# Sixteen copies of cached values ahead of the first head group, weight loads in halves, and a new set of early products in a one-core residual stack

## The chip, the core and the metric

The kernel runs on one core of a Trainium2 chip, as one program in one launch. The metric is the device time of that launch in microseconds (us), the median over several runs. All arithmetic is 32-bit float.

## The reference

Four residual layers are applied in turn to `x`, 64 sequences of 32 positions with 512 features:

```python
# per-sequence channel mix, weights picked by itok_B_0_15
x = x + einsum('bct,bcd->bdt', x, L0_weights[cond])
# linear layer with a LoRA, picked by itok_B_6_15
h = einsum('bsd,brd->bsr', x, A[adapter])
x = x + (einsum('bsd,od->bso', x, base_w) + bias + einsum('bsr,bor->bso', h, B[adapter]))
# attention over a paged cache: 32 query heads, 8 key/value heads of 128, 16 pages of 32 keys
q, k, v = x @ Wq.T, x @ Wk.T, x @ Wv.T
q, k = rope(rmsnorm(q)), rope(rmsnorm(k))
keys = concat(k_cache[block_table], k); values = concat(v_cache[block_table], v)
p = softmax(where(valid, q @ keys.T * SCALE, -1e30))   # a cached key is valid below cache_seqlen
x = x + (p @ values) @ Wo.T
# per-sequence channel mix once more
x = x + einsum('bct,bcd->bdt', x, L3_weights[cond])
```

A sequence has 512 cached keys and 32 new ones, and every key/value head serves four query heads.

## The kernel before

**Tiles and groups.** The 2048 positions are 16 tiles of 128 rows, four sequences to a tile. The eight key/value heads are two groups of four (`g` is 0 or 1), and the attention runs over all tiles for group 0 and then for group 1. A *unit* is one sequence and one group, 128 units in all. A unit has four *periods* (the code calls them slots), one for each key/value head, so there are n = 512 periods. Eight units, that is two tiles or 32 periods, are a *pair*; pairs 0 to 7 are group 0, pairs 8 to 15 group 1.

**A plan written by hand.** Each piece of work is put into a period with `at(slot, where, ...)`, and `slot(i)` sends the pieces of a period out in a fixed order: "fetch", "pool", scores, transpositions of the probabilities, "pe", "power", "turn", values, "dve", "keep", "act", "store". Each engine works through its own instructions in that order. SyncE (SP) issues the ordinary transfers and GpSimd (POOL) the indirect ones, also in program order.

**A period of attention.** `Unit.scores` multiplies the queries of one head by all keys (L808, L811). One instruction on VectorE (DVE) adds the mask `pen` and takes the minimum, `top` (L816). ScalarE (ACT) takes the exponential (L827), and `divide` scales it (L833). `Unit.flip` transposes the probabilities (L850) and DVE copies them out of PSUM (L852). `Unit.values` multiplies them by the values three periods behind the scores (L863). The masks are made on POOL by `Unit.mask` (L779), for a unit three periods ahead of its first score.

**Where keys and values come from.** `Turn` takes 128 cached keys of one group, transposes them on PE, and `Turn.store` writes them to DRAM page by page (`kT_dram`). For group 0 the sixteen turns lie in front, for group 1 one turn goes with each tile of group 0. For group 1, `Turn.store` also copies the values of its 128 cached rows into `v_dram`, in which a row holds the values of all four heads of the group (L281). A unit's keys come as sixteen ordinary transfers of one page each (L759). Its values come as indirect loads of 128 rows each (`gather`, L105), four times 128 keys. In group 1 that is one gather of 512 numbers per row from `v_dram`. In group 0 there are two gathers per 128 keys, each of 256 numbers per row (one pair of heads), from the cache as it came in; their row numbers are the tables `rows["pair", 0]` and `rows["pair", 1]`, made in front. The table for group 1 is made in the middle (`second_rows`). The loaded values have eight buffers (`v_sb`), two units' worth.

**Projections beside the attention.** During pair i the projections of pair i+1 run on the same PE: `Plain.project` for keys and values (L555), `Block.project` for the queries (L622, by a scheme of seven products for eight), whose weight sums are made by `block_sum` on DVE. `Norm` normalizes and rotates the heads; its `power` step runs on POOL (L679) and waits for DVE's `ss` (L677).

**Front.** The first two layers (`First`) run tile by tile before and beside the projections of pair 0. Their x tiles are loaded on SP (L382), from `begin`, the first period of all. The weights of group 0 are loaded there as well: v's and k's after the second x tile's place in the plan, and all of q's at once behind the second period.

**Weights.** The weight buffers `w0` to `w8` are used three times: for group 0, for group 1 (loaded during pair 7) and for the output weights wo (loaded during pair 15). The loads are whole tiles of 1 MB (k's and v's as two of 512 KB), put at the start of a period ("fetch").

**End.** The output projection also forms seven products for eight, per pair of tiles: p1 to p7, each of 16 matmuls with 256 columns. For the first pair of tiles three of them, p1, p2 and p7, are made early, spread over the last 24 periods (`early_product`, L1110); their inputs `o_in` are loaded 27 periods before the end, all four at once, and `early_sums` combines them on DVE. The rest is made behind the periods (L1281), with the last channel mix (`mixed`) of a pair behind the next pair's p1.

## Time and profile before

| | us |
|---|---|
| median of 3 runs (2548.47 to 2557.93) | 2554.17 |
| profiled execution, its own time | 2682.29 |
| its span, first to last instruction | 2680.5 |
| PE busy in the span | 2522.0 (94%) |
| DVE busy | 1663.5 (62%) |
| POOL busy | 1331.2 (50%) |
| ACT busy | 1287.0 (48%) |
| start of the first score matmul | 207.1 |
| start of group 1's first score matmul | 1319.6 |
| gathers of group 0's values, 512 | 519.0 |
| gathers of group 1's values, 256 | 261.3 |

Busy time is the sum over an engine's instructions. A row of a group names line, engine, operation, tiles (written <- read) and count, then busy time and mean ns of one, then the idle time before these instructions and what ended it. The span of the one profiled execution is longer than the median of the runs without a profile by 126 us; sums in this document that are made from its rows are compared with its own time.

### The profile page before, as it was taken

To read this page: it belongs to the slowest core of one execution; us is meant where nothing else is said; L and a number is where in the kernel's file an instruction comes from. 1 tells how busy PE (TensorE), PEld (TensorE's weight loads), DVE (VectorE), ACT (ScalarE), POOL (GpSimd) and SP (SyncE) were. 2 spreads that over 40 slices of the span, in tenths; PEclk is the share of its full clock that TensorE was granted. 3 is DMA by queue.
4 is the path that set the end of the run, shared out by engine and by line. 5 is a ranking of instruction groups with operands and counts; after the bars stand their busy time and mean duration, and the time that the engine had idled before them with its cause. 6 is when DMAs were issued, how large, how long until landed. Compare 5 with 4: busy or idle time off the path is not lost.

```text
span 2680.5 us, 47052 instructions
## 1 busy us (share of the span) xinstructions
PE 2522.0 (94%) x13824; PEld 1882.3 (70%) x13824; DVE 1663.5 (62%) x4166; ACT 1287.0 (48%) x3671; POOL 1331.2 (50%) x1136
## 2 busy tenths in 40 slices
PE   6998999999999898989899999999999989999999
PEld 3555666666666666666677777777777767888888
DVE  5655666566666666667667767776777766522322
ACT  1235555556555555556566666666666654100000
POOL 4326666666667666667654555554544544100000
PEclk9999999999999999999999999999999999999999
DMA  7746565556565656575556555665656675323321
GB/s 244 246 155 181 158 183 156 170 163 180 160 179 158 181 154 200 183 218 158 173 167 193 170 180 170 182 181 171 199 167 202 210 264 171 143 79 115 123 79 56
DMA packets 441023, 457.34 MB, mean 171 GB/s; under 512 B 54081, under 2 KB 366273, under 8 KB 430401
## 3 DMA queue, kind: packets, MB, share of 16 engines
q1 hardware_dynamic: 393408, 315.35, 37.6%
q0 software_dynamic: 47360, 138.99, 17.8%
q8 instruction: 112, 1.84, 0.3%
q14 instruction: 143, 1.16, 0.1%
HBM read 382.82 MB, written 75.50 MB: 171 GB/s over the span
## 4 chain that ended last, share of the span: by engine, by line
PE 83%; DVE 6%; DMA 4%; issue 3%; another core or an unknown queue 2%; ACT 2%; SPq 1%; POOL 1%; DVEq 0%; ACTq 0%; POOLq 0%
PE o_ps L863 15%; PE proj_ps L622 14%; PE out_ps L1281 14%; PE s_ps L808 9%; PE proj_ps L555 8%; PE pT_ps L850 7%; PE s_ps L811 7%; PE head_ps L721 2%; PE o_ps L875 2%; PE l_ps L461 2%; DVE pT L852 1%; DVE sm L816 1%; DMA x_sb<-in_x 1%; DVE raw L634 1%
## 5 line engine op out<-in xcount | busy, mean ns | idle before, releaser
L816 DVE CUSTOM_DVE_ANT_0 sm<-s_ps,pen 128x544 f32<-128x544 f32 x512 | 370.5, 724 | 534.3 <-PE s_ps L811 284.8
L863 PEld LDWEIGHTS o_ps<-pT,v_sb 128*128 128x128 f32 x4096 | 526.0, 194 | 148.7 <-issue 135.2
L827 ACT ACTIVATE sm<-sm,top 128x544 f32<-128x544 f32 x512 | 383.5, 749 | 499.1 <-DVE top L816 418.6
L105 POOL DMA_INDIRECT v_sb<-in_kv_cache,pair_rows x512 | 519.0, 1014 | 198.5 <-issue 119.2
L863 PE MATMUL o_ps<-pT,v_sb 128*128 128x128 f32 x4096 | 547.7, 277 | 8.5 <-DMA v_sb<-in_kv_cache,pair_rows 5.3
L833 ACT ACTIVATE sm<-sm,share 128x512 f32<-128x512 f32 x512 | 370.8, 724 | 227.9 <-DVE share L832 190.4
L105 POOL DMA_INDIRECT v_sb<-v,v_rows x256 | 261.3, 1021 | 270.3 <-PE o_ps L863 220.6
L808 PE MATMUL s_ps<-kT,qT 128*128 128x288 f32 x1024 | 351.9, 425 | 36.7 <-DVE top L816 26.3
L852 DVE COPY pT<-pT_ps 128x512 f32<-128x512 f32 x512 | 351.7, 687 | 52.8 <-PE s_ps L811 21.1
L679 POOL TENSOR_TENSOR rstd<-ss,minus_half 128x4 f32<-128x4 f32 x160 | 187.2, 1170 | 383.0 <-DVE ss L677 379.0
L850 PE MATMUL pT_ps<-ident,sm 128*128 128x128 f32 x2048 | 310.6, 275 | 22.0 <-DVE pT L852 15.7
L850 PEld LDWEIGHTS pT_ps<-ident,sm 128*128 128x128 f32 x2048 | 255.5, 141 | 80.4 <-DVE pT L852 15.6
L811 PE MATMUL s_ps<-kT,qT 128*128 128x256 f32 x1024 | 306.3, 381 | 1.7 <-DMA kT<-kT 1.2
L779 POOL TENSOR_SCALAR pen<-key_f,seq_f 128x544 f32<-128x544 f32 x128 | 280.3, 2190 | 13.5 <-DMA x<-xS 2.6
L811 PEld LDWEIGHTS s_ps<-kT,qT 128*128 128x128 f32 x1024 | 195.1, 191 | 57.4 <-DMA kT<-kT 2.3
L105 POOL DMA_INDIRECT mix_rows<-in_w,cond_rows x32 | 40.8, 1275 | 333.3 <-DVE mix_diag L168 293.0
L672 ACT ACTIVATE sq<-raw 128x128 f32<-128x128 f32 x640 | 190.7, 301 | 32.3 <-DVE raw L634 21.6
L808 PEld LDWEIGHTS s_ps<-kT,qT 128*128 128x128 f32 x1024 | 155.5, 192 | 59.4 <-DVE top L816 32.0
L634 DVE TENSOR_TENSOR raw<-proj_ps,raw 128x512 f32<-128x512 f32 x224 | 150.7, 685 | 27.8 <-PE proj_ps L622 25.9
L1281 PE MATMUL out_ps<-w,o_in 128*128 128x256 f32 x768 | 167.1, 379 | 0.0
L1331 ACT COPY p<-out_ps 128x256 f32<-128x256 f32 x7 | 2.6, 373 | 333.1 <-PE out_ps L1281 333.1
L1281 PEld LDWEIGHTS out_ps<-w,o_in 128*128 128x128 f32 x768 | 145.9, 190 | 19.8
(159 smaller groups left out, 3592.9 us busy)
## 6 DMA issues: line engine op xcount, KB each, us to landing
kT<-kT SPq DMA_DIRECT2D x2048, 64.0 KB
o<-oT SPq DMA_DIRECT2D x32, 1024.0 KB
o_in<-o SPq DMA_DIRECT2D x32, 1024.0 KB
rot<-rot SPq DMA_DIRECT2D x48, 256.0 KB
wq<-in_wq SPq DMA_DIRECT2D x8, 1024.0 KB
page_rows<-in_kv_cache SPq DMA_DIRECT2D x32, 256.0 KB
vn<-v_rows SPq DMA_DIRECT2D x32, 256.0 KB
kT<-page_T SPq DMA_DIRECT2D x32, 256.0 KB
```

The costliest lines, as they stand in the source:

```text
L105: nc.gpsimd.indirect_dma_start(out=dst, out_offset=None, in_=table, in_offset=bass.IndirectOffsetOnAxis(ap=index, axis=0),)
L622: nc.tensor.matmul(self.ps, lhsT=self.pair.x[x][:, half][:, c, :], rhs=blocks(self.b)[w][:, c, :], start=(c == 0), stop=(c == 1),)
L779: nc.gpsimd.tensor_scalar(self.pen, key_f, seq_f[:, self.b : self.b + 1], BIG, ALU.is_ge, ALU.mult)
L808: nc.tensor.matmul(ps[:, first:HID], lhsT=q, rhs=self.kT[:, :n1, k, :], start=True, stop=True)
L811: nc.tensor.matmul(ps[:, HID : first + LA], lhsT=q, rhs=self.kT[:, n1:, k, :], start=True, stop=True)
L816: nc.vector.tensor_tensor_reduce(out=sm, in0=ps[:, first : first + LA], in1=self.pen, scale=1.0, scalar=3e38, op0=ALU.add, op1=ALU.min, ac ...
L827: nc.scalar.activation(sm, sm, AF.Exp, bias=top, scale=-1.0, accum_out=total)
L833: nc.scalar.activation(sm[:, :L], sm[:, :L], AF.Copy, scale=share)
L850: nc.tensor.transpose(ps[:, c, :], self.sm[k][:, c * P : (c + 1) * P], ident)
L852: nc.vector.tensor_copy(pT, ps)
L863: nc.tensor.matmul(self.o_ps[k], lhsT=self.v[c][:, k * D : (k + 1) * D], rhs=self.pT[k][:, c, :], start=(c == 0), stop=False,)
L1281: nc.tensor.matmul(ps[:, :HALF], lhsT=o[:, i, :], rhs=w[i // REP][:, i % REP, :], start=(i == 0), stop=(i == KG * REP - 1),)
```

## The change

**Values.** `v_dram` becomes a list of two, and `Turn.store` makes its copy for both groups. So sixteen copies of 256 KB, from the cache to DRAM, come into the front, each ahead of its turn's store of keys. `fetch_values` makes one gather of 512 numbers per row in either group, with one table of row numbers, `v_rows`, made in front; `second_rows` and the two tables for group 0 go.

**Front.** It begins one period later relative to pair 0 (the number 11 becomes 10). The first five x tiles are loaded in the first three periods, two in each. v's weights come with the second period, k's with the third, q's by halves in the following eight.

**Weight loads.** Every weight tile is loaded by two transfers of 512 KB, one per period, at a period's end ("store"). The starts are periods 6, 11, 21, 23, 32, 34, 36 and 38 of the pair's plan (before: 6, 11, 21, 21, 32, 32, 32, 32). The block sums move by one to three periods.

**Last periods.** The three early products are now the p1 of three pairs of tiles, (1, 2, 0) in this order, all with the same output weights w11. Their inputs are loaded by halves, one per period; four of the six tiles loaded are for pair 0, one for each of the others. The third weights are made 19 to 22 periods into the last 24 (before: 8 to 11). The sums of pair 0 are made behind the periods, where pairs 0, 1 and 2 now have six products each and the others seven.

```diff
...
-    def load_kv_weights(g, kind):
-        w = wpool.tile([P, NC, KG * D], F32, name=f"w{'kv'[kind]}{g}", tag=f"w{kind}")
-        for i in (0, 1):
-            nc.sync.dma_start(
-                out=w[:, :, i * 2 * D : (i + 1) * 2 * D],
-                in_=wkv[2 * g + i][:, :, kind * 2 * D : (kind + 1) * 2 * D],
+    def load_kv_weights(g, kind, i):
+        if i == 0:
+            w_sb[kind] = wpool.tile(
+                [P, NC, KG * D], F32, name=f"w{'kv'[kind]}{g}", tag=f"w{kind}"
             )
-        w_sb[kind] = w
-    def load_q_weights(g, k):
-        w_sb["q", k] = wpool.tile([P, NC, REP * D], F32, name=f"wq{g}_{k}", tag=f"w{2 + k}")
-        nc.sync.dma_start(out=w_sb["q", k], in_=wq[KG * g + k])
-    def load_o_weights(k):
-        tag = f"w{(1, 0, 2, 3, 4, 5, 6, 7)[k]}"
-        w_sb["o", k] = wpool.tile([P, REP, HID], F32, name=f"wo{k}", tag=tag)
-        nc.sync.dma_start(out=w_sb["o", k], in_=wo[k])
+        nc.sync.dma_start(
+            out=w_sb[kind][:, :, i * 2 * D : (i + 1) * 2 * D],
+            in_=wkv[2 * g + i][:, :, kind * 2 * D : (kind + 1) * 2 * D],
+        )
+    def load_q_weights(g, k, i):
+        if i == 0:
+            w_sb["q", k] = wpool.tile([P, NC, REP * D], F32, name=f"wq{g}_{k}", tag=f"w{2 + k}")
+        part = slice(i * NC // 2, (i + 1) * NC // 2)
+        nc.sync.dma_start(out=w_sb["q", k][:, part], in_=wq[KG * g + k][:, part])
+    def load_o_weights(k, i):
+        if i == 0:
+            tag = f"w{(1, 0, 2, 3, 4, 5, 6, 7)[k]}"
+            w_sb["o", k] = wpool.tile([P, REP, HID], F32, name=f"wo{k}", tag=tag)
+        part = slice(i * REP // 2, (i + 1) * REP // 2)
+        nc.sync.dma_start(out=w_sb["o", k][:, part], in_=wo[k][:, part])
...
-    v_dram = dram.tile([PAGES * PSIZE, KG * D], F32, name="v_1")
+    v_dram = [dram.tile([PAGES * PSIZE, KG * D], F32, name=f"v_{g}") for g in range(NG)]
...
-                if self.g:
-                    nc.sync.dma_start(
-                        out=v_dram[c * P : (c + 1) * P, :].rearrange("k (i f) -> k i f", i=2),
-                        in_=self.cached(1),
-                    )
+                nc.sync.dma_start(
+                    out=v_dram[self.g][c * P : (c + 1) * P, :].rearrange("k (i f) -> k i f", i=2),
+                    in_=self.cached(1),
+                )
...
-                if self.g:
-                    gather(v, v_dram[:, :], rows["v"][:, at])
-                else:
-                    by_pair = kv_cache.rearrange("r (w f) -> (r w) f", w=2)
-                    for i in (0, 1):
-                        gather(v[:, i * 2 * D : (i + 1) * 2 * D], by_pair, rows["pair", i][:, at])
+                gather(v, v_dram[self.g][:, :], v_rows[:, at])
...
-                at(home - 11, "fetch", make, pair_of, 0, Pair, 0)
+                at(home - 10, "fetch", make, pair_of, 0, Pair, 0)
...
-                sums = [(b, what) for b in (0, 1) for what in (3, 2, 1)] + [(0, 4), (1, 4)]
-                for w, one in enumerate(sums):
-                    at(home + 4 + w, "dve", block_sum, *one)
+                sums = [(b, what) for b in (0, 1) for what in (3, 2, 1, 4)]
+                for w, one in zip((5, 6, 7, 9, 10, 11, 12, 13), sums):
+                    at(home + w, "dve", block_sum, *one)
             if p == NT // 2 - 1:
-                last = g == NG - 1
-                if last:
+                if g == NG - 1:
                     loads = [(load_o_weights, k) for k in range(2 * KG)]
                 else:
                     loads = [(load_kv_weights, g + 1, k) for k in (1, 0)]
                     loads += [(load_q_weights, g + 1, k) for k in range(KG)]
-                for w, load in zip((6, 11, 21, 21, 32, 32, 32, 32), loads):
-                    at(home + w, "fetch", *load)
+                for w, load in zip((6, 11, 21, 23, 32, 34, 36, 38), loads):
+                    for j in (0, 1):
+                        at(home + w + j, "store", *load, j)
...
-        begin = -WINDOW - AHEAD - 11
+        begin = -WINDOW - AHEAD - 10
...
-            home = -WINDOW - AHEAD - 7 + 2 * t
+            home = -WINDOW - AHEAD - 6 + 2 * t
             f = [first_of, t]
-            at(max(begin, home - 5), "fetch", make, *f, First, t)
+            at(home - 5 if t > 4 else begin + t // 2, "fetch", make, *f, First, t)
...
-        def second_rows():
-            rows["v"] = rows_of(const, "v_rows", table, B * NC, PSIZE, lane32_f, tag="rows_0")
-        at(n // 2 - 2, "dve", second_rows)
...
-        def fetch_o(name, g, t):
-            o = o_pools[0].tile([P, KG * REP, P], F32, name="o_in", tag=name)
-            nc.sync.dma_start(out=o, in_=o_dram[g][t])
-            early[name] = o
+        def fetch_o(name, g, t, i):
+            if i == 0:
+                early[name] = o_pools[0].tile([P, KG * REP, P], F32, name="o_in", tag=name)
+            part = slice(i * KG * REP // 2, (i + 1) * KG * REP // 2)
+            nc.sync.dma_start(out=early[name][:, part], in_=o_dram[g][t][:, part])
-        def early_sums(i):
-            a11, a12, a21, a22 = (early[f"a{i}"] for i in (11, 12, 21, 22))
+        def early_product(pair, name, i):
             if i == 0:
-                early["s3"] = wpool.tile([P, KG * REP, P], F32, name="s3", tag="w8")
-            dst, a, op, b = (
-                (early["s3"], a11, ALU.subtract, a21),
-                (a21, a21, ALU.add, a22),
-                (a11, a21, ALU.subtract, a11),
-                (a12, a12, ALU.subtract, a11),
-            )[i]
-            nc.vector.tensor_tensor(dst, a, b, op)
-        def early_product(name, o, first, half, i):
-            if i == 0:
-                early[name] = ps_m.tile([P, HID], F32, name="proj_ps", tag="m")[:, : HID // 2]
+                early["p1", pair] = ps_m.tile([P, HID], F32, name="proj_ps", tag="m")
             nc.tensor.matmul(
-                early[name],
-                lhsT=early[o][:, i, :],
-                rhs=w_sb["o", first + i // REP][:, i % REP, half * HID // 2 : (half + 1) * HID // 2],
+                early["p1", pair][:, : HID // 2],
+                lhsT=early[name][:, i, :],
+                rhs=w_sb["o", i // REP][:, i % REP, : HID // 2],
                 start=(i == 0),
                 stop=(i == KG * REP - 1),
             )
-        def early_keep(name):
-            ps = early[name]
-            early[name] = o_pools[0].tile([P, HID // 2], F32, name=f"{name}_first")
-            nc.scalar.copy(early[name], ps)
+        def early_keep(pair):
+            ps = early["p1", pair]
+            early["p1", pair] = o_pools[0].tile([P, HID // 2], F32, name=f"p1_{pair}")
+            nc.scalar.copy(early["p1", pair], ps[:, : HID // 2])
-        for j, (name, o, k, half) in enumerate(
-            (("p1", "a11", 0, 0), ("p2", "a12", KG, 0), ("p7", "s3", 0, 1))
-        ):
+        for j, (pair, name) in enumerate(((1, "a12"), (2, "a21"), (0, "a11"))):
+            for i in (0, 1):
+                at(home - 3 + 3 * j + i, "store", fetch_o, name, 0, 2 * pair, i)
             for i in range(KG * REP):
-                at(home + 8 * j + i // 2, "pe", early_product, name, o, k, half, i)
-            at(home + 8 * j + 7, "act", early_keep, name)
+                at(home + 8 * j + i // 2, "pe", early_product, pair, name, i)
+            at(home + 8 * j + 7, "act", early_keep, pair)
+        for i in (0, 1):
+            at(home + 9 + i, "store", fetch_o, "a12", 1, 0, i)
+            at(home + 12 + i, "store", fetch_o, "a22", 1, 1, i)
+            at(home + 17 + i, "store", fetch_o, "a21", 0, 1, i)
         for k in range(KG):
-            at(home + 8 + k, "dve", third_weights, k)
-        for i, w in enumerate((5, 13, 15, 17)):
-            at(home + w, "dve", early_sums, i)
+            at(home + 19 + k, "dve", third_weights, k)
...
-            load_kv_weights(0, 1)
-            load_kv_weights(0, 0)
             for i in range(begin + 1, begin + 11):
                 slot(i)
                 for _ in range(2 if i < begin + 6 else 1):
                     next(more, None)
-                if i == begin + 1:
-                    for k in range(KG):
-                        load_q_weights(0, k)
+                c = i - begin - 1
+                if c < 2:
+                    for j in (0, 1):
+                        load_kv_weights(0, 1 - c, j)
+                elif c < 10:
+                    load_q_weights(0, (c - 2) // 2, c % 2)
...
-                    for k in (0, 1):
-                        base = 2.0 * k * PAGES * PSIZE + 1
-                        rows["pair", k] = rows_of(
-                            const, f"pair_rows_{k}", table, B * NC, PSIZE, lane32_f, 2.0, base,
-                            tag=f"rows_{k}",
-                        )
+                    v_rows = rows_of(const, "v_rows", table, B * NC, PSIZE, lane32_f)
...
-                    for name, g, t in (
-                        ("a11", 0, 0), ("a12", 1, 0), ("a21", 0, 1), ("a22", 1, 1)
-                    ):
-                        fetch_o(name, g, t)
...
-                if pair:
+                p1 = early.get(("p1", pair))
+                if p1 is None:
                     p_1 = product(a11, w11)
                     p1 = pool.tile([P, HALF], F32, name="p1")
-                    nc.vector.tensor_tensor(s3, a11, a21, ALU.subtract)
-                    add(a21, a21, a22)
-                    nc.vector.tensor_tensor(a11, a21, a11, ALU.subtract)
-                    for at_last in waiting:
-                        mixed(*at_last)
-                    p_2 = product(a12, w21)
-                    nc.vector.tensor_tensor(a12, a12, a11, ALU.subtract)
-                    p_7 = product(s3, w_3)
-                    p_3 = product(a12, w22)
-                else:
-                    p1, p_2, p_7 = early["p1"], early["p2"], early["p7"]
-                    p_3 = product(a12, w22)
+                nc.vector.tensor_tensor(s3, a11, a21, ALU.subtract)
+                add(a21, a21, a22)
+                nc.vector.tensor_tensor(a11, a21, a11, ALU.subtract)
+                for at_last in waiting:
+                    mixed(*at_last)
+                add(x3[0][:, lo], x3[0][:, lo], p1)
+                add(x3[0][:, hi], x3[0][:, hi], p1)
+                p_2 = product(a12, w21)
+                nc.vector.tensor_tensor(a12, a12, a11, ALU.subtract)
+                add(x3[0][:, lo], p_2, x3[0][:, lo])
+                p_7 = product(s3, w_3)
+                if pair == 0:
...
-                add(x3[0][:, lo], x3[0][:, lo], p1)
-                add(x3[0][:, hi], x3[0][:, hi], p1)
-                add(x3[0][:, lo], p_2, x3[0][:, lo])
...
+                p_3 = product(a12, w22)
                 add(x3[0][:, hi], p_3, x3[0][:, hi])
...
```

## The prediction

> **What bounds the kernel now.** I read the engine shares first: PE is busy 94% of the span, so the question is where the other time goes. The stretches between the starts of the pairs' first score matmuls (found by L808) tell. A pair is 32 periods, the same work sixteen times over; pairs 0 to 7 are the first group, 8 to 15 the second. Columns: stretch, length, then busy us and count of PE, its weight loads, DVE, ACT, POOL; last the granted clock, DMA share and GB/s.
>
> ```profile
> 484.00:622.00 138.00, 127.77 (x722) 92.68 (x721) 89.86 (x238) 79.39 (x227) 93.12 (x83) 0.98 0.57 168
> 1032.40:1178.80 146.40, 128.50 (x723) 92.15 (x721) 88.56 (x235) 79.22 (x227) 94.03 (x84) 0.98 0.64 198
> 1682.40:1803.10 120.70, 120.61 (x714) 89.80 (x713) 89.19 (x234) 77.04 (x225) 62.22 (x51) 1.00 0.61 179
> 2044.60:2170.50 125.90, 120.60 (x710) 89.53 (x709) 88.33 (x234) 77.27 (x225) 64.20 (x53) 0.99 0.69 216
> 2170.50:2291.80 121.30, 108.99 (x699) 93.44 (x698) 75.70 (x181) 59.23 (x133) 44.53 (x36) 0.95 0.61 197
> ```
>
> See that pair 11 (third row) is PE alone: 120.6 of 120.7 us. Pair 2 (first row) needs 138 for the same products. Only POOL differs, 93 us against 62. The eight first-group pairs take 1319.6 - 207.1 = 1112.5 us; pairs 8 to 13 take 725.0, 120.8 each.
>
> POOL's waits in pair 2, then in pair 11 (engine, tile, line waited for: us, times, longest):
>
> ```profile
> POOL rstd L679 <- DVE ss L677: 18.1, 7, 4.2
> POOL v_sb L105 <- issue: 14.8, 51, 0.3
> POOL v_sb L105 <- PE o_ps L863: 10.3, 4, 9.0
> ...
> POOL v_sb L105 <- PE o_ps L863: 23.2, 12, 7.9
> ```
>
> And the groups of POOL in pair 2:
>
> ```profile
> L105 POOL DMA_INDIRECT v_sb<-in_kv_cache,pair_rows x64 | 64.4, 1006 | 27.4 <-issue 14.8 <-PE o_ps L863 10.3 <-PE pT_ps L850 1.3
> L779 POOL TENSOR_SCALAR pen<-key_f,seq_f 128x544 f32<-128x544 f32 x8 | 17.3, 2167 | 0.7
> ```
>
> Per unit (four periods, 15.1 us at PE's pace) POOL issues 8 gathers of 1.006 us with 14.8 / 64 = 0.23 us between, 9.9 us, one mask `pen` of 2.17 and 1.4 `rstd` of 1.15: 13.6 us. It runs in order, so its 18.1 us of waits for DVE's `ss` (2.3 per unit) count: 15.9 us. That is more than PE needs. POOL falls behind, `pen` comes late behind gathers, and the softmax reduction on DVE waits for it:
>
> ```profile
> 503.24 2.10 POOL L779 TENSOR_SCALAR pen<-key_f,seq_f 128x544 f32<-128x544 f32 x1
> 504.75 0.72 DVE L816 CUSTOM_DVE_ANT_0 sm<-s_ps,pen 128x544 f32<-128x544 f32 x1 [3.97 <-remote]
> ```
>
> DVE stood 3.97 us for nothing but this mask. PE then stands too, and its clock halves for 3.4 or 6.8 us after several such gaps (clock 0.98).
>
> **Part 1: one gather per 128 keys.** 256 of 512 gathers go from group 0: per unit 4 x (1.006 + 0.23) = 4.9 us off POOL, leaving about 8.7 plus waits, as in group 1, whose gathers of twice the row are no dearer (1.021 against 1.006 us). What is late next is PE. Group 0 keeps one page transposition per tile that group 1 lacks: 8 of 0.11 us per pair, so 120.7 + 0.9 = 121.6, times 8 = 973 us; 4 us for the reload stretch: 977. Saved: **135 us** of the profiled run.
>
> What it adds: 16 copies of 256 KB from DRAM to DRAM in front, on SP, each between a `page_rows` load and a `kT` store. Group 1's like copies issue in 0.62 us and move in some 2.5 us. In the instruction order each SP transfer waits for the one eight before it. SP has room there (the last kT store issues at 171, the first kT load at 190.6), and DMA is 0.57 busy from 100 to 218; 4 MB more adds about 0.12. Hidden, I cost it at 0. If all 16 issues came onto the path: 10 us. The first gather waits for all 16 copies, but the last is planned ten periods earlier.
>
> **Part 2: the front.** In the first 45 us PE waits for an x tile queued behind 6 MB of weights:
>
> ```profile
> 37.53 2.05 PE L407 MATMUL mix_ps<-x_sb,mix_diag 128*128 128x512 f32 x2 [8.56 <-DMA x_sb<-in_x]
> ```
>
> Now x tiles 2 and 3 issue before the weights, which come at 1 MB a period and later 0.5. The 8.6 us go, and with them the half clock behind (three groups run 2.6 us longer than their equals at 47 us): **-11 us**. The front is one period shorter, but the same products merely overlap differently: 0. The weights are still early: v's are needed some 40 us in. Cover gone: one 0.5 MB part, some 3 us. The row numbers move from four times 16 to one set of 8 small DVE instructions in front and none in the middle: under 2 us, 0. The block sums move by one to three periods on DVE, ahead of their first use: 0 (bounds -3 to +3).
>
> **Part 3: loads in halves, one per period, at the period's end.** At 2120 and 2165 bursts of 2 and 4 MB fill the DMA engines (1.01 busy, 365 and 417 GB/s); kT, v and v_new transfers queue behind. PE is busy 6.67 of 10 us at 2165, 5.72 at 2195, 5.59 at 2215. Pair 6 loses 146.4 - 138 = 8.4 us to q's burst (counted in part 1), pair 14 some 4 of its 5, pair 15 more. Against halves stands a rule: the Trainium skill, "DMA: Bandwidth & Descriptors", section Bandwidth, wants transfers of 1 MiB or more, and its anatomy section gives each about 2.0 us fixed. Twenty 1 MB loads cut in two would by that cost up to 20 x 2 = 40 us. The row says otherwise for this place: eight transfers are in flight, so fixed parts overlap, and it is a saturated stretch (1.01) that PE suffers from. I take 0 for the cut. A steady period needs 0.61 x 3.77 = 2.3 us of DMA; 0.5 MB at the 365 GB/s of the burst adds 1.4: 3.7 of 3.77. It just fits.
>
> **Part 4: the last periods.** Early products stay 48 matmuls of 256 columns, now p1 of three pairs; four third weights stay, the four 2.28 us DVE sums move behind the loop; o_in grows from 4 to 6 MB. Without projections, pair 15's last six units ran at best 13.2 us; the first two carry the wo loads, and at 3.7 us of DMA a period can't go under 15: 30 + 6 x 13.3 = 110, against 121.3: **-11**; pair 14 **-4**. Behind the loop the 53 products stay 53 (48 + 5 before; 6 + 6 + 6 + 35 now). DVE of pair 0: three sums end 6.9 us in, a12 waits for p_2, w_2 is there some 18 us in, needed at 21. For pairs 1 and 2 a mix has no p_1 before it: 2 x 0.7. Also a22 lands 5.3 us after p_4 ended (2374.3 to 2379.59); two DVE sums, four smaller, then a12 gives 14.2 us, while p_3 is due after mix, p_2, p_7 at 16.2. It holds by 2 us. **+1.5**.
>
> **Sum.** -135 - 11 - 4 - 11 + 1.5 = -159.5: span 2521, own time 2523 (2682.3 before).
>
> **From the profiled run to the median.** The profiled run is 2682.3, the median 2554.2: 128 us less, with no record of where. Group 1 and the tail can hardly be shorter without the profiler: PE is full there. Group 0's surplus over PE's pace is 139.5, near 128; POOL, with a thin overload (15.9 against 15.1), is where a slightly dearer instruction costs most. So I believe that most of the surplus exists only while profiled, and the changed kernel's profiled run and median come close. If all 128 lie in POOL's overload, the median after is 2523; if half lies elsewhere (front, latencies), 2523 - 64 = 2459. Nearer the first, since PE-bound stretches can hide little: I take 15 elsewhere, **2508 us**, 1.8% faster; its own range 2490 to 2530.
>
> **Rivals.**
> - B, the surplus is largely real without the profiler: about half, so 2459. For: overload follows from instruction times, whoever looks. Against: 128 us must then come from stretches where PE is full.
> - C, nothing to gain: group 0 already runs at PE's pace unprofiled (surplus 139.5 - 128 = 11), and the front and end gains are lost to the 2 MB more of o_in and the saturated periods: 2554 - 9 = 2545. For: 128 so near 139.5. Against: the front's 8.6 us and the bursts are waits for DMA, not for POOL.
> - D, the copies in front, slower: if each of the 16 holds SP for issue and movement (0.62 + 2.5 = 3.1 us) and the kT stores behind it pace the front, 50 us are added. On 2523 that is 2573. It decides from 31 / 16 = 1.9 us per copy on. For: SP is in order and eight transfers deep. Against: SP's 19 us of room and PE-bound periods in front.
>
> **Chances.** Forecast 0.65, B 0.18, C 0.10, D 0.07. Range 2460 to 2535: the forecast's, B's upper half, the edge of C. A measurement of this kernel can tell 0.5% from no change (2541.4 and 2566.9 are the bounds). Faster 0.83, same 0.10, slower 0.07.
>
> **What would show it.** Right: group 0's pairs at 120 to 123 us with POOL near 62; 512 v gathers of 1.02 us; no wait of `sm` for `pen`; first scores near 196 us; a profiled run within 30 us of the median. Wrong: pairs of group 0 above 126 (SP or DMA then, not POOL); first scores after 207 (copies); pair 15 not under 118 (DMA at its limit). A median above 2541 with group 0 at 121 means that the surplus was the profiler's alone.

## The result, and the profile after

| | before | after |
|---|---|---|
| median, nine runs each | 2550.21 us (2547.69 to 2557.93) | 2543.38 us (2539.27 to 2547.76, and one of 4298.66) |
| profiled execution, own time / span | 2682.29 / 2680.5 us | 2539.27 / 2537.5 us |
| first score matmul at | 207.1 | 198.9 |
| pairs 0 to 7 | 1112.5 | 974.6 |
| pairs 8 to 13 | 725.0 | 724.8 |
| pair 14, pair 15 | 125.9, 121.3 | 120.2, 128.1 |
| behind the periods | 388.7 | 390.9 |

The run of 4298.66 us had a granted clock of 0.558, against 0.993 to 0.996 in the other eight, and the ratio leaves it out. The ratio of the timed runs is 0.9966, with a 95% interval of 0.9953 to 0.9979: 0.3% faster, less than the 0.5% that the prediction named as the least that can be told from no change. 2508 was forecast, and the range ended at 2535; the time lies above both. The two profiled executions differ by 143 us. Why one pair of numbers says 7 and the other 143 was the main question of the runs below.

The stretches of the changed kernel, for the same pairs as before (2, 7, 11, 14, 15; columns as above: stretch, length, PE, PEld, DVE, ACT, POOL, then clock, DMA share, GB/s):

```profile
439.90:561.50 121.60, 121.51 (x722) 90.71 (x721) 88.73 (x234) 78.01 (x227) 61.83 (x51) 1.00 0.65 191
1048.00:1173.50 125.50, 121.98 (x722) 90.69 (x721) 97.47 (x242) 78.08 (x226) 64.54 (x51) 1.00 0.68 205
1656.80:1777.60 120.80, 120.71 (x715) 89.89 (x715) 89.03 (x234) 77.10 (x225) 62.18 (x51) 1.00 0.60 180
1898.30:2018.50 120.20, 119.43 (x710) 89.18 (x709) 88.74 (x234) 76.50 (x224) 61.98 (x50) 1.00 0.69 210
2018.50:2146.60 128.10, 108.63 (x695) 92.97 (x694) 71.10 (x179) 58.87 (x133) 45.58 (x39) 0.92 0.70 219
```

Pair 2 is PE alone now, 121.5 of 121.6 us, with POOL at 62 instead of 93. Pair 14 is PE alone too. Pair 15 is the exception: PE stands 128.1 - 108.6 = 19.5 us in it, against 12.3 before, and its clock is 0.92.

The group of all value gathers, and the longest waits of POOL and of DVE (us, times, longest):

```profile
L105 POOL DMA_INDIRECT v_sb<-v,v_rows x512 | 523.3, 1022 | 494.3 <-PE o_ps L862 397.3
```

```profile
POOL v_sb L105 <- PE o_ps L862: 397.3, 174, 18.9
...
DVE sm L815 <- PE s_ps L810: 466.9, 436, 7.7
```

Half as many gathers for group 0, at 1.02 us each instead of 1.01, and POOL waits for PE to give buffers back. DVE's reduction `sm` waits for PE's scores and, but for 3.4 us in all, for nothing else.

### The profile page after: what moved, and what is told of

Read it like the earlier page. It is cut to its first block, busy times and chain, and to the rows that moved or that the text cites. A ratio compares the mean times of both kernels' runs of the same rounds, so it can differ in the third digit from the quotient of the medians.

```text
span 2537.5 us, 46802 instructions
## 1 busy us (share of the span) xinstructions
PE 2473.9 (97%) x13824; PEld 1869.8 (74%) x13824; DVE 1665.4 (66%) x4150; ACT 1280.2 (50%) x3669; POOL 1072.5 (42%) x880
## 4 chain that ended last, share of the span: by engine, by line
PE 87%; DVE 3%; DMA 2%; ACT 1%; SPq 1%; issue 1%; ACTq 0%; DVEq 0%
PE o_ps L862 17%; PE out_ps L1256 14%; PE proj_ps L626 14%; PE s_ps L807 10%; PE proj_ps L559 8%; PE s_ps L810 8%; PE pT_ps L849 8%; PE head_ps L725 3%; PE o_ps L874 2%; DMA o<-oT 1%; PE l_ps L465 1%; DVE sm L815 1%; DVE rot_a L717 1%; PE proj_ps L1093 1%; PE mix_ps L1274 1%
## 5 line engine op out<-in xcount | busy, mean ns | idle before, releaser
L105 POOL DMA_INDIRECT v_sb<-v,v_rows x512 | 523.3, 1022 | 494.3 <-PE o_ps L862 397.3
L862 PEld LDWEIGHTS o_ps<-pT,v_sb 128*128 128x128 f32 x4096 | 520.7, 192 | 137.3 <-issue 134.5
L683 POOL TENSOR_TENSOR rstd<-ss,minus_half 128x4 f32<-128x4 f32 x160 | 193.7, 1210 | 473.5 <-DVE ss L681 472.2
L807 PE MATMUL s_ps<-kT,qT 128*128 128x288 f32 x1024 | 347.4, 421 | 10.3 <-DMA kT<-kT 10.1
L105 POOL DMA_INDIRECT mix_rows<-in_w,cond_rows x32 | 32.7, 1022 | 347.7 <-DVE mix_diag L168 301.0
L833 DVE TENSOR_SCALAR p_new<-sm,share 128x32 f32<-128x32 f32 x512 | 148.6, 290 | 18.2
```

The costliest lines, as they stand in the source:

```text
L105: nc.gpsimd.indirect_dma_start(out=dst, out_offset=None, in_=table, in_offset=bass.IndirectOffsetOnAxis(ap=index, axis=0),)
L807: nc.tensor.matmul(ps[:, first:HID], lhsT=q, rhs=self.kT[:, :n1, k, :], start=True, stop=True)
L862: nc.tensor.matmul(self.o_ps[k], lhsT=self.v[c][:, k * D : (k + 1) * D], rhs=self.pT[k][:, c, :], start=(c == 0), stop=False,)
```

## Experiments

Each kernel ran beside the kernel before, on one chip per section. The number of the chip is given, because the results turned out to depend on it.

### Chip 6: the kernel before again, and the parts alone

**before_again** is the kernel before, unchanged.

> The kernel before, once more, with a new profile. Theory S (the slow first group, 138 us a pair, belonged to that one profiled execution; in the timed runs PE already sets the pace): timed 2550, and if the profile is an ordinary execution, a span near 2550 with pairs of group 0 at 121 to 124 us. Theory P (the profiler itself slows POOL's gathers): timed 2550, but the profiled span again near 2680 with pairs at 137 to 139 us. Theory R (the slow pairs are in the timed runs as well, and the change loses elsewhere what it gains there): timed 2550 with the profiled span within 20 us of it and pairs of group 0 still clearly over 125 us.

Measured: 2679.82 us (2670.52 to 2689.29, 22 executions), and 2683.63 for 43 executions of the same kernel beside it. Every one of the 22 has a span of 2669 to 2688 us and a clock of 0.983 to 0.987. So the profiled execution's 2682 was no outlier: recorded like all of these, the kernel before takes that long on this chip. None of the three theories had that, since all expected 2550 for the timed runs.

**gather_only** is part 1 without the rest.

```diff
-    v_dram = dram.tile([PAGES * PSIZE, KG * D], F32, name="v_1")
+    v_dram = [dram.tile([PAGES * PSIZE, KG * D], F32, name=f"v_{g}") for g in range(NG)]
...
-                if self.g:
-                    gather(v, v_dram[:, :], rows["v"][:, at])
-                else:
-                    by_pair = kv_cache.rearrange("r (w f) -> (r w) f", w=2)
-                    for i in (0, 1):
-                        gather(v[:, i * 2 * D : (i + 1) * 2 * D], by_pair, rows["pair", i][:, at])
+                gather(v, v_dram[self.g][:, :], rows["v"][:, at])
```

> The kernel before with part 1 alone: one gather per 128 keys in group 0 and the sixteen copies in front. Theory S: 2540 to 2552, the gain at most the few us that group 0 stands over 121.6 a pair. Theory R: 2420 to 2460. If the copies hold the front up, over 2555, with the first scores after 212 us in its profile.

Measured: 2547.92 us, ratio 0.9498 [0.9466, 0.9531]. Its pair 2:

```profile
450.20:571.80 121.60, 121.52 (x723) 90.72 (x722) 88.94 (x234) 77.88 (x227) 61.69 (x51) 1.00 0.65 191
```

Part 1 alone takes 136 us away on this chip (2683.63 - 2547.92). First scores start at 207.0 us; without the copies they start between 204.6 and 207.4 in the traces with the old front. The sixteen copies cost nothing that shows against this spread.

**front_only** is part 2 with whole weight loads: x tiles first, weights behind them, the front one period shorter.

```diff
-            at(max(begin, home - 5), "fetch", make, *f, First, t)
+            at(home - 5 if t > 4 else begin + t // 2, "fetch", make, *f, First, t)
...
-            load_kv_weights(0, 1)
-            load_kv_weights(0, 0)
...
+                c = i - begin - 1
+                if c < 2:
+                    load_kv_weights(0, 1 - c)
+                elif c < 10 and c % 2 == 0:
+                    load_q_weights(0, (c - 2) // 2)
```

> The kernel before with part 2 alone: x tiles ahead of the weights, one period less, the weights as whole tiles one by one. Theory S and R alike: first scores 8 to 11 us earlier, 2539 to 2544. If the front was bound by something else: no change.

Measured: 2679.75 us, ratio 0.9976 [0.9958, 0.9994]; first scores at 200.1, 4.5 us earlier than in before_again on this chip and 7 earlier than in the first trace of the kernel before. Group 0's pairs stay at 136 to 144 us.

**pairs_both** puts the two gathers into group 1 as well: the suspected cost doubled.

```diff
-                if self.g:
-                    gather(v, v_dram[:, :], rows["v"][:, at])
-                else:
+                if True:
```

> The kernel before with two gathers per 128 keys in group 1 too (256 more gathers on POOL). Theory S: POOL's overload is not there in timed runs, so 2550 to 2570. Theory R or a POOL at its limit in every run: +70 to +140 us, 2620 to 2690.

Measured: 2811.1 us, ratio 1.0472 [1.043, 1.0514]. Group 1's pairs go from 120.7 us to between 134 and 140, and the run is 127 us longer than the kernel before beside it, within the 70 to 140 of theory R. Wherever two gathers fetch 128 keys, a pair costs some 16 us more on this chip.

### Chip 7: the changed kernel again, and its end

**before_c2** is the kernel before, **after_c2** the changed kernel, both unchanged.

> The kernel before on this chip, for its profile. Theory V (the pace of group 0 belongs to the chip: POOL's two gathers per 128 keys take longer on one than on another): either 2680 with 137 to 139 us a pair, or 2550 with 121 to 124 us, and in the second case its v gathers or the gaps between them are shorter in the profile than the 1.01 and 0.23 us of the first profile. Theory S (one odd execution) fell with before_again, so 2680 with pairs of 121 us would be a surprise.

> The changed kernel on this chip. Theory V: 2540 to 2547 whatever the chip, because PE sets the pace of both groups; against the kernel before it is then 0.995 to 0.998 on a chip of the fast kind and 0.945 to 0.955 on one of the slow kind.

Measured: 2679.34 (and 2680.93 beside it) against 2549.01, ratio 0.9508 [0.9487, 0.9529]. Here the change is worth 5%.

**old_end** keeps the loads in halves and takes back the early products of the kernel before.

```diff
-        for j, (pair, name) in enumerate(((1, "a12"), (2, "a21"), (0, "a11"))):
+        for j, (name, o, k, half) in enumerate(
+            (("p1", "a11", 0, 0), ("p2", "a12", KG, 0), ("p7", "s3", 0, 1))
+        ):
...
-            at(home + 19 + k, "dve", third_weights, k)
+            at(home + 8 + k, "dve", third_weights, k)
+        for i, w in enumerate((5, 13, 15, 17)):
+            at(home + w, "dve", early_sums, i)
```

> The changed kernel with the early products of before (p1, p2 and p7 of the first pair of tiles, their sums and third weights in the middle of the last 24 periods), o_in still loaded by halves. If the 2 MB more of o_in and the DVE work at the very end cost what pair 15 lost: pair 15 at 112 to 119 us instead of 128 and the time 8 to 15 us below the changed kernel. If the halves themselves (eight wo halves in eight periods) are at fault: pair 15 stays over 124.

Measured: 2542.33 us, pair 14 at 121.2, pair 15 at 125.2, the rest behind the periods 388.4. Pair 15 does not come back to 121.

**spread_end** keeps the new products, but spreads the last loads over more periods and makes the third weights earlier.

```diff
+                if g == NG - 1:
+                    starts = (6, 11, 21, 23, 32, 34, 40, 46)
...
-                at(home - 3 + 3 * j + i, "store", fetch_o, name, 0, 2 * pair, i)
+                at(home + (-3, 2, 9)[j] + i, "store", fetch_o, name, 0, 2 * pair, i)
...
-            at(home + 9 + i, "store", fetch_o, "a12", 1, 0, i)
-            at(home + 12 + i, "store", fetch_o, "a22", 1, 1, i)
+            at(home + 13 + i, "store", fetch_o, "a12", 1, 0, i)
+            at(home + 20 + i, "store", fetch_o, "a22", 1, 1, i)
...
-            at(home + 19 + k, "dve", third_weights, k)
+            at(home + (0, 2, 6, 12)[k], "dve", third_weights, k)
```

> The changed kernel with the wo and o_in halves of the last pair spread over 32 periods, and the third weights earlier. If crowded transfers are what pair 15 waits for: pair 15 at 108 to 118 us, the time 10 to 20 us below the changed kernel, near 2528. If the amount (10 MB beside kT and v) is at fault, whatever its spread: over 122.

Measured: 2544.78 us (2535.71 to 2549.28); pair 15 in its stretch:

```profile
2022.60:2144.00 121.40, 107.62 (x698) 92.26 (x698) 72.33 (x179) 59.23 (x133) 46.10 (x39) 0.94 0.73 231
```

PE stands 13.8 us of pair 15 instead of 18.2 (after_c2), with more bytes per us moved. That fits crowded loads as the cause of 4.4 us of pair 15's idle time, unless it was the third weights, which moved too; thirds_early below speaks against these. Pair 15 does not fall to the 108 to 118 us that this cause was expected to give, and the medians of the two kernels lie 4 us apart with overlapping ranges. So it is likely, and not shown.

### Chip 8: is it POOL's throughput?

**pen_dve** is the kernel before with its masks made on DVE, so POOL loses some 17 us of work per pair and keeps its gathers.

```diff
-                nc.gpsimd.tensor_scalar(
+                nc.vector.tensor_scalar(
...
-            at(KG * (u - 1) + 1 if u else -1, "pool", call, unit_of, u, "mask")
+            at(KG * (u - 1) + 1 if u else -1, "dve", call, unit_of, u, "mask")
```

> The kernel before with the masks made on DVE and not on POOL; both gathers per 128 keys stay. Theory POOL (its own time, 15.9 us per unit against PE's 15.1, holds group 0): POOL falls to some 13.7 us per unit, pairs of group 0 go from 138 to 121 to 125 us, the time to 2550 to 2590. Theory landing (the gathers land late, whatever POOL does beside them): 133 to 138 us a pair, over 2640.

Measured: 2684.44 us, ratio 1.0016 [0.9997, 1.0036]. Its pair 2, and then a piece of its time line (start, length, engine and line; in brackets the idle time before):

```profile
487.20:627.90 140.70, 128.08 (x722) 92.66 (x721) 91.30 (x242) 78.40 (x226) 74.54 (x75) 0.96 0.57 165
```

```profile
504.15 0.59 PE L811 MATMUL s_ps<-kT,qT 128*128 128x256 f32 x2
504.29 0.95 POOL L105 DMA_INDIRECT v_sb<-in_kv_cache,pair_rows  x1 [0.30 <-PE o_ps L863]
505.54 0.95 POOL L105 DMA_INDIRECT v_sb<-in_kv_cache,pair_rows  x1 [0.31 <-issue]
506.80 0.95 POOL L105 DMA_INDIRECT v_sb<-in_kv_cache,pair_rows  x1 [0.30 <-issue]
508.05 0.95 POOL L105 DMA_INDIRECT v_sb<-in_kv_cache,pair_rows  x1 [0.30 <-issue]
510.65 0.72 DVE L816 CUSTOM_DVE_ANT_0 sm<-s_ps,pen 128x544 f32<-128x544 f32 x1 [6.54 <-remote]
```

POOL is busy 74.5 of 140.7 us and the pair is as slow as ever: POOL's throughput was not the cause, and with the mask on DVE itself, neither was a late `pen`. The second view shows what stands in its place. The scores are done at 504.74, DVE has nothing else to do, and the reduction starts at 510.65, after a row of gathers that ran back to back; the last of them ended at 509.00. The profile knows no releaser ("remote"). ACT and PE then wait for DVE.

Call a reduction late when it starts over 0.6 us after the end of its scores and of DVE's instruction before it. In pen_dve, 57 of group 0's 256 reductions are late, 117 us in sum, and 5 of group 1's (4 us). In before_c2 the numbers are 61 (106 us) and 5 (5 us); in gather_only, with one gather per 128 keys in both groups, they are 4 and 5. So late reductions go with the second gather.

**gather_front** is parts 1 and 2 with whole loads and the old end (first diff, against the changed kernel). **thirds_early** is the changed kernel with the third weights eleven periods earlier (second diff). **after_c3** is the changed kernel.

```diff
-                for w, load in zip((6, 11, 21, 23, 32, 34, 36, 38), loads):
-                    for j in (0, 1):
-                        at(home + w + j, "store", *load, j)
+                for w, load in zip((6, 11, 21, 21, 32, 32, 32, 32), loads):
+                    at(home + w, "fetch", *load)
```

```diff
-            at(home + 19 + k, "dve", third_weights, k)
+            at(home + 8 + k, "dve", third_weights, k)
```

> The kernel before with parts 1 and 2: one gather per 128 keys, x tiles ahead of the weights, one period less; whole loads and the early products of before. If the front's 7 to 9 us stay and the end of before is no worse than the new one: 2536 to 2542, 3 to 8 us below the changed kernel. If the halves are worth their place: at or above the changed kernel.

> The changed kernel with its third weights 8 to 11 periods into the last 24, as before the change. If DVE's work in the last five periods costs time: 3 to 5 us less than the changed kernel, all between the last score and the tail's products. If the transfers alone hold pair 15: within 1.5 us of it.

> The changed kernel, for comparison on this chip: 2540 to 2550. The kernel before beside it: theory V (a matter of the chip) allows 2550 on some chip; if it is 2670 to 2700 on a third one as well, the nine runs near 2550 stand alone.

Measured: gather_front 2541.55 (2539.19 to 2545.13), thirds_early 2543.52 (2542.27 to 2547.89), after_c3 2546.11 (2541.75 to 2549.55); against the kernel before 0.9485, 0.95 and 0.95. Parts 1 and 2 alone do as well as the whole change, by the medians better by 4.6 us, which these few executions can't settle. thirds_early has pair 15 at 127.0 (after_c3: 126.0): the third weights are not what holds pair 15.

gather_front and old_end have the same early products; one loads whole weights, the other halves. Their pairs 14 and 15 take 125.9 and 121.8 us against 121.2 and 125.2, together 247.7 against 246.4. So the halves mostly move a wait from pair 14 to pair 15.

### Chip 3: the loss is absent

**double_gather** is gather_only, values of both groups laid out by key, but with two gathers of 256 numbers per 128 keys. The text on record below speaks of group 0; the changed line serves group 1 as well, so both groups have two gathers.

```diff
-                gather(v, v_dram[self.g][:, :], rows["v"][:, at])
+                by_pair = v_dram[self.g].rearrange("r (w f) -> (r w) f", w=2)
+                for i in (0, 1):
+                    gather(v[:, i * 2 * D : (i + 1) * 2 * D], by_pair, rows["pair", i][:, at])
```

**bufs10** is the kernel before with ten value buffers. **no_early** is gather_front without early products, their loads and their sums; all of pair 0's products come behind the periods. **after_c4** is the changed kernel.

```diff
-                v = room["v"].tile([P, KG * D], F32, name="v_sb", bufs=8)
+                v = room["v"].tile([P, KG * D], F32, name="v_sb", bufs=10)
```

```diff
-                at(home + 8 * j + i // 2, "pe", early_product, name, o, k, half, i)
-            at(home + 8 * j + 7, "act", early_keep, name)
...
-            at(home + 8 + k, "dve", third_weights, k)
-        for i, w in enumerate((5, 13, 15, 17)):
-            at(home + w, "dve", early_sums, i)
+            at(n - 12 + 2 * k, "dve", third_weights, k)
...
-                        fetch_o(name, g, t)
```

> Group 0's values are laid out by key in DRAM, as in the changed kernel, but each 128 keys are still fetched by two gathers of 256 columns. Count theory (two gathers in a row on POOL hold up DVE's score reduction): group 0 stays at 136 to 141 us a pair, total 2670 to 2690, ratio to before 0.997 to 1.003. Source theory (gathers straight from the input's cache are what is slow): group 0 at 121 to 123 us, total 2543 to 2553, ratio near 0.95. Something between says that both count.

> Ten v_sb buffers instead of eight in the kernel before, nothing else. If the gathers come too late for PE (latency), two more buffers let POOL run a quarter unit further ahead: group 0 falls under 132 us a pair, total under 2640. If streaks of gathers that block DVE are what costs, more free buffers give longer streaks: group 0 138 to 146 us, total 2680 to 2740. If neither: within 0.3% of before.

> One gather per 128 keys and the changed front, weights whole, and no early product, no early o_in load and no early sum in the last periods (48 matmuls of 256 columns and their o_in loads move behind the loop; no part of the result changes). Tail +20 to +23 us, to 409 to 412. If pair 15 waits for the loads and sums of the early products: pair 15 falls from 122 to 128 us to 90 to 101, total 2533 to 2543. If it waits for the 8 MB of wo loads alone: pair 15 at 105 to 118, total 2548 to 2562.

> The changed kernel again, beside the others on this chip: 2543 to 2550, group 0 at 121.6 us a pair, pair 15 at 126 to 129, tail 391. The kernel before beside it: if what makes it slow here is the chip, near 2550 on some chip; if it is the recorded execution, 2675 to 2685 again.

Measured, beside 2553.19 us for 32 executions of the kernel before: double_gather 2541.97 (0.9957 [0.9944, 0.997]), bufs10 2552.82 (0.9995 [0.9981, 1.0008]), no_early 2545.22 (0.9968 [0.9957, 0.998]), after_c4 2542.0 (0.9956 [0.994, 0.9972]).

This chip shows no loss: the kernel before takes 2553, and these executions were recorded like those on the other chips. So neither of the first two could answer its question, but their traces show the kernel before's gathers on a chip where they cost nothing. bufs10, pairs 6 and 7:

```profile
938.10:1066.10 128.00, 123.79 (x723) 91.94 (x722) 88.58 (x234) 78.00 (x227) 95.27 (x85) 0.98 0.73 229
1066.10:1195.70 129.60, 124.47 (x722) 92.60 (x722) 99.30 (x250) 78.10 (x226) 94.75 (x82) 0.98 0.62 187
```

Its pairs 1 to 5 take 121.1 us each, with POOL as busy as in the slow trace (93.8). bufs10 stands in for the kernel before, whose time it shares; with after_c4, stretch by stretch, it gives the change's account on such a chip:

| stretch | bufs10 | after_c4 | gain |
|---|---|---|---|
| up to the first scores | 206.2 | 200.4 | 5.8 |
| pair 0 | 126.2 | 119.4 | 6.8 |
| pairs 1 to 5 | 605.7 | 608.0 | -2.3 |
| pair 6 | 128.0 | 121.6 | 6.4 |
| pair 7 | 129.6 | 125.1 | 4.5 |
| pairs 8 to 13 | 724.3 | 724.8 | -0.5 |
| pair 14 | 123.2 | 120.1 | 3.1 |
| pair 15 | 119.9 | 126.5 | -6.6 |
| behind the periods | 388.6 | 390.9 | -2.3 |
| span | 2551.7 | 2536.9 | 14.8 |

Pair 7's gain has a cause of its own. DVE in the last unit of bufs10's pair 7, time line:

```profile
1184.43 0.25 DVE L148 TENSOR_SCALAR v_rows_f<-ints_sb,lane_f 128x64 f32<-128x64 int32 x1
...
1188.78 0.19 DVE L151 TENSOR_SCALAR v_rows<-v_rows_f 128x64 int32<-128x64 f32 x1 [4.10 <-DMA v_sb<-in_kv_cache,pair_rows]
...
1190.83 3.01 PE L555 MATMUL proj_ps<-wv,x_a 128*128 128x512 f32 x4 [4.46 <-DVE raw L634]
```

`second_rows` writes group 1's row numbers into the buffer `rows_0`, which group 0's last gather still reads. The write waits until that gather has landed, everything behind it on DVE waits too, and PE stands 4.46 us. That unit takes 21.7 us here and 23.3 in the first trace of the kernel before, where the same write waited 3.47 us; with the table made in front it takes 15.3. The line of before:

```profile
1312.68 0.20 DVE L151 TENSOR_SCALAR v_rows<-v_rows_f 128x64 int32<-128x64 f32 x1 [3.47 <-DMA v_sb<-in_kv_cache,pair_rows]
```

no_early answers for pair 15:

```profile
2028.60:2131.20 102.60, 89.18 (x595) 74.21 (x594) 66.55 (x175) 57.58 (x129) 44.49 (x37) 0.96 0.73 231
```

```profile
1899.40:2019.50 120.10, 119.34 (x711) 88.97 (x710) 88.14 (x232) 75.83 (x222) 60.98 (x50) 1.00 0.68 209
2019.50:2146.00 126.50, 106.09 (x695) 91.04 (x694) 71.73 (x180) 59.35 (x133) 45.81 (x39) 0.93 0.71 222
```

The first fence is no_early's pair 15, the second after_c4's pairs 14 and 15. Pair 15 is 24 us shorter than in the changed kernel (126.5 to 102.6), between the two ranges expected: PE does 17 us less there and stands 7 us less (13.4 against 20.4). But no_early also loads whole weights; gather_front on chip 8, which loads them whole too and keeps the early work, has pair 15 at 121.8, so the early work accounts for some 19. Behind the periods that work costs 415.1 - 388.7 = 26.4 us, more than the 20 to 23 expected. The early products are worth doing only as far as they fill gaps. They do so little: no_early takes 2545.22, the changed kernel beside it 2542.0.

### Chip 12: the same two kernels where the loss is present

> As double_gather, because on its chip the kernel before lost nothing in group 0 and the question could not be asked. If the kernel before beside it stands near 2680: the count theory (two gathers in a row hold up DVE's reduction on such a chip, whatever they read) expects group 0 at 136 to 141 us a pair, 2670 to 2690, reductions late by over 0.6 us 40 to 60 times; the source theory (reading the input's cache is what is slow) 121 to 123 us, 2540 to 2553. If the kernel before stands near 2553: 2540 to 2546 for both.

> As bufs10, asked again. If the kernel before beside it stands near 2680: late gathers as the cause expect under 132 us a pair and under 2640; streaks that hold up DVE expect 138 to 146 us and 2680 to 2740. If the kernel before stands near 2553: within 0.3% of it.

Measured, beside 2683.04 us for the kernel before: double_gather_2 2800.59 (2798.06 to 2801.09), ratio 1.0432 [1.0392, 1.0473]; bufs10_2 2684.61, ratio 1.0013 [0.999, 1.0035]. Above the 2670 to 2690 expected, because both groups have two gathers: 135 to 141 us in pairs of either group. Where the values are read from doesn't matter here; how many gathers fetch them does. Two more buffers change nothing: the time is neither that of gathers that land too late nor that of longer rows of gathers.

The same program on two chips, pair 3, first double_gather (chip 3), then double_gather_2 (chip 12):

```profile
574.50:695.70 121.20, 121.20 (x723) 90.72 (x722) 88.74 (x234) 78.04 (x227) 94.03 (x83) 1.00 0.65 192
```

```profile
615.50:751.40 135.90, 126.40 (x722) 91.76 (x721) 88.19 (x234) 78.51 (x226) 94.10 (x84) 0.99 0.58 171
```

POOL's busy time is the same to 0.1 us, DVE's to 0.6; PE's is 5.2 us longer on chip 12. The first difference is in when DVE starts. Time lines of POOL and DVE's reduction, chip 3 and then chip 12:

```profile
510.97 0.95 POOL L105 DMA_INDIRECT v_sb<-v,pair_rows  x1 [0.30 <-issue]
510.99 0.59 PE L807 MATMUL s_ps<-kT,qT 128*128 128x256 f32 x2
511.62 0.72 DVE L812 CUSTOM_DVE_ANT_0 sm<-s_ps,pen 128x544 f32<-128x544 f32 x1 [0.85 <-PE s_ps L807]
512.23 0.95 POOL L105 DMA_INDIRECT v_sb<-v,pair_rows  x1 [0.30 <-PE pT_ps L846]
```

```profile
491.67 0.59 PE L807 MATMUL s_ps<-kT,qT 128*128 128x256 f32 x2
491.89 0.95 POOL L105 DMA_INDIRECT v_sb<-v,pair_rows  x1 [0.30 <-issue]
493.14 0.94 POOL L105 DMA_INDIRECT v_sb<-v,pair_rows  x1 [0.30 <-issue]
494.39 0.95 POOL L105 DMA_INDIRECT v_sb<-v,pair_rows  x1 [0.30 <-issue]
495.40 0.72 DVE L812 CUSTOM_DVE_ANT_0 sm<-s_ps,pen 128x544 f32<-128x544 f32 x1 [4.97 <-PE o_ps L859]
```

On chip 3 the reduction starts in the middle of a gather, 0.04 us after its scores end at 511.58. On chip 12 it starts 3.14 us after its scores ended (492.26), just behind a gather. All 512 reductions of a trace, sorted by the gather that runs (or has just ended) when they come due, counted in a row of gathers less than 0.4 us apart; each entry gives how many are late:

| gather in its row | double_gather, chip 3 | double_gather_2, chip 12 | pen_dve, chip 8 |
|---|---|---|---|
| none running | 0 of 126 | 9 of 174 | 1 of 224 |
| first | 0 of 114 | 0 of 92 | 0 of 124 |
| second or third | 0 of 134 | 22 of 152 | 4 of 97 |
| fourth or later | 0 of 138 | 78 of 94 | 57 of 67 |

So on chips 12 and 8 it is long rows of gathers behind which reductions start late; on chip 3 the same rows do nothing. The late ones of chip 12 add up to 215 us, beside the 257 us between the two spans. That is no exact account: a late reduction need not delay the end by as much, and PE's busy time in the whole trace is also 91 us longer (2564.7 against 2474.0), at a granted clock of 0.978 against 0.995.

What a late reduction waits for can be read from the trace's records of semaphores, the signals by which one engine tells another that a piece of work is done. On chip 3, 99% of PE's instructions that signal, from 200 to 2150 us, have a signal of PE recorded within 0.1 us of their end (double_gather). On chip 12 it is 49% (double_gather_2). In the stretch of pen_dve shown above, PE's scores are done at 504.74, but PE's signals are recorded at 506.32, 507.72, 509.15 and 510.58, some 1.4 us apart, and three others follow within 0.15 us. The reduction starts in their midst, at 510.65. Of the 109 late reductions on chip 12, 107 start within 0.1 us after a recorded signal of PE. So what is late is the signal, as far as the records go; some are missing, and which one is which can't be told.

Why that is so on these chips stays open. The Trainium skill, "SBUF — State Buffer", section "SBUF: two separate sides", tells of a pair of ports that DVE and GpSimd share, held by one for a whole instruction while the other is blocked. That looks like this picture at first. But it names DVE instructions with two inputs in SBUF or in a two-port mode, and the reduction reads its scores from PSUM and only `pen` from SBUF. Also the reduction in pen_dve starts 1.65 us after the last gather ended, and the rule would hold on chip 3, where the same program shows nothing of it.

Another rival is the recording itself. For the same changed kernel, with 3190 PE instructions that signal, the record holds 3188 of PE's signals on chip 3 (after_c4) and 2769 on chip 7 (after_c2). All executions on chips 6, 7, 8 and 12 come with a span and a clock, that is, they were recorded. So it isn't known whether the loss is there without a recording. Recording alone does not make it, as chip 3 shows, but a chip on which recording holds up the signals would look the same.

## Why the prediction was wrong, step by step

- **Group 0 at PE's pace: right.** 120.7 + 0.9 = 121.6 was forecast and 121.6 measured; pairs 0 to 7 take 974.6 for 977.
- **The reason for it: wrong.** "That is more than PE needs": 15.9 us of POOL per unit against 15.1. The step counted POOL's waits for `ss` as work that can't be made up, although POOL's own view showed 10.3 us in which it waited for PE to give buffers back. pen_dve takes the masks away and gains nothing; bufs10 carries the same 93.8 us of POOL per pair at PE's full pace. The reduction's wait of 3.97 us was misread as well. The mask shown beside it is written from 503.24 to 505.34, but the reduction starts at 504.75, so it can't have waited for that mask. In the whole trace of before it waits for a mask once (us, times, longest):

```profile
DVE sm L816 <- POOL pen L779: 0.9, 1, 0.9
```

  That one gather per 128 keys would bring group 0 to PE's pace was right, then, but by luck: it was the number of gathers, and not POOL's total time.
- **From the profiled run to the median: the step that failed.** "Most of the surplus exists only while profiled" put 128 us down to the profiler. On chip 3 all executions are recorded and the kernel before takes 2553; on chips 6, 7, 8 and 12, recorded too, it takes 2678 to 2684. The two numbers that were shown belong, then, to different kinds of chip. For the nine timed runs that is inferred: their chip isn't listed, and their ratio of 0.9966 fits chip 3's 0.9956 and none of the others' 0.95. For the two profiled executions the records speak: the first trace of before holds 2729 of 3193 signals of PE, like those of chips 6, 7, 8 and 12 (2683 to 2783), that of the changed kernel 3189 of 3190, like those of chip 3 (3163 to 3188). So the 143 us between the two profiles compare two kinds of chip. On a chip without the loss little of the 139.5 us is there to be saved: bufs10's pairs 0 to 7 take 989.5 us on chip 3, 17 more than eight times 121.6. "I take 15 elsewhere" was the term: it took the median down by 15 us, and in fact the median lies 4 us above the profiled run. By the prediction's last sign (a median above 2541 with group 0 at 121) the surplus would be the profiler's alone; chip 3's recorded executions rule that out as the whole cause, while a part in it on the other chips stays open.
- **The front, -11: right in kind, 8.2 measured** (4.5 to 7 in front_only, 5.8 on chip 3). **Copies at 0: right**, 207.0 in gather_only.
- **Row numbers "in the middle: under 2 us, 0": wrong on the good side.** Eight small instructions cost 1.8 us of DVE, but the first write waited for a gather, and the unit took 6.4 us longer. The idle time was in the trace of before, at the last unit of pair 7 (the 3.47 us above).
- **Pair 14, -4: right** (5.7, on chip 3 3.1), but pair 15 gave it back: together the two took 247.2 us before and 248.3 after. The 40 us that stood against halves did not come; the section of the Trainium skill from which the prediction took the 2.0 us is about transfers that GpSimd issues, and these go out on SP.
- **Pair 15, -11: wrong, +6.8.** The sum took 3.7 us of DMA for a period of 3.77, and "it just fits". It didn't. The 2.3 us of a steady period are an average, in which stores of 1 MB of o come all at once, and the o_in loads beside the weights grew to 6 MB. The chain of waits through pair 15 shows it (start, us, what), then SP's time line:

```profile
2029.84 11.29 DMA o<-oT
...
2047.67 7.86 DMA o_in<-o
...
2093.62 10.41 DMA o<-oT
...
2109.81 5.28 DMA kT<-kT
```

```profile
2029.84 0.33 SPq L897 DMA_DIRECT2D o<-oT  x1
2030.96 15.65 SPq L763 DMA_DIRECT2D kT<-kT  x16
2046.66 0.90 SPq L203 DMA_DIRECT2D wo<-in_wo  x2
2047.67 0.36 SPq L1083 DMA_DIRECT2D o_in<-o  x1
```

  Sixteen key loads, which elsewhere go out in some 10 us, take 15.65 behind a store of 1 MB and the halves. Against the changed kernel on the same chip, spread_end takes 4.4 us of PE's idle time back with its loads spread, and no_early 7 us with the early ones dropped and the weights whole. That accounts for part of pair 15 only.
- **"The four DVE sums move behind the loop": wrong in fact.** Three of them start in the last periods, beside the third weights (at 2134.86, 2138.30 and 2146.35). The stretch around the end of the periods:

```profile
2135.00:2150.00 15.00, 11.18 (x78) 9.23 (x77) 14.16 (x21) 5.63 (x13) 0.00 (x0) 1.00 0.00 0
```

  DVE is busy 14.16 of 15 us there, and PE 11.18. With the third weights moved away, thirds_early shortens what follows by 1 us and pair 15 not at all.
- **The tail, +1.5: right**, 2.2.

The profiled own time was forecast at 2523 and came at 2539.3: 18 us of that from pair 15, 3 from the front, less some 5 from the pairs before it. The other 19 of the 35 us are the step to the median, 15 and 4. The rival "nothing to gain" (2545) had the number, and its first half fits that kind of chip: group 0 already ran near PE's pace. Its reason, the profiler alone, is not borne out by chip 3, and it was held at 0.10.

No version beats the changed kernel with any certainty. gather_front (2541.55 beside 2546.11) is simpler and not slower. On a chip that shows the loss, one gather per 128 keys is what matters. All kernels that have it take 2541 to 2549 us on the four chips where they ran. Those with two in one group or both take 2542 to 2553 on chip 3 and 2678 to 2811 on the others.

## What to carry to other kernels

When a profiled execution and the timed runs differ by more than a part of a per cent, first ask whether they ran on the same chip, and run the old kernel again beside its trace, before an explanation is built on the profiler. An execution that isn't recorded, on that chip, would settle the rest. An engine whose busy time and waits add up to more than the bound isn't proved to be the bound: take work off it and see. A buffer reused for a small table can stop a whole engine until the slowest reader of the old content has landed.

## What the runs showed of the hardware

- Recorded executions of one program differ by 5% between chips (2553 against 2680 us), those of another by 10% (2542 against 2801). POOL's and DVE's busy times are the same (1581 and 1661 against 1586 and 1659 us in the second pair of traces); PE's is 91 us longer, at a granted clock of 0.978 against 0.995. What the loss grows with is the number of indirect gathers on POOL.
- On such a chip a DVE reduction that comes due in the fourth or a later gather of a row starts late 78 times in 94, in the first gather of a row 0 times in 92 (double_gather_2). In pen_dve's stretch it starts 5.9 us after the scores that it waits for have ended, among signals of PE that are recorded only then.
- A gather of 128 rows costs POOL 1.00 to 1.01 us for 256 numbers per row and 1.02 to 1.03 for 512, with 0.30 between two in a row. For these two sizes the cost is per gather and hardly per byte.
